# A list scheduler that counts results of other engines as ready somewhat later, with new due times

## The chip, the cores and the metric

The kernel runs on one core of a Trainium2 chip. A core has five engines that run side by side and wait for each other through semaphores: TensorE (PE in the profile; its weight loads are PEld), VectorE (DVE), ScalarE (ACT), GpSimd (POOL) and SyncE (SP), which here issues nearly all DMA transfers. The metric is the time of one execution on the device in microseconds, as the median of several runs.

## The reference

Four graph layers work on 128 graphs of 64 nodes, with 256 features a node, all in float32. Each layer adds to `x` a function of the normalized and rectified `h = max(layernorm(x), 0)`.

```python
# layers 0 and 1: attention of 8 heads over each graph; layer 0 masks, layer 1 adds log(adj + 1e-6)
attn = softmax(q @ k.T / sqrt(32) [masked or + log(adj + 1e-6)])
x = x + (attn @ v) @ Wo + bo
# layer 2: five rounds of a gated graph network
for l in range(5):
    m   = h @ weight[l]
    agg = A.T @ m                       # A = adj != 0, per graph
    h   = gru(agg, h)                   # gates r, z, n from 256 -> 768 products of agg and of h
x = x + h * mask
# layer 3: gated sum of a product along the graph and one beside it
f   = norm * (adj @ ((h @ theta) * norm))
g   = sigmoid(h @ W_t + b_t)
x   = x + elu(g * f + (1 - g) * (h @ W_h))
```

## The kernel before

**Tiling.** Two graphs make a tile of 128 rows (a pair), four pairs a group, and there are 16 groups. Activations of a group lie transposed, as two blocks of 128 features by 512 nodes. Products of 256x256 matrices are done with seven block products instead of eight (`by_seven`, `gru`, `seven_products`): sums of blocks are formed ahead on POOL or DVE, and each product's bank in PSUM is read by DVE or ACT before the next product goes into it. A second version of the whole network stands behind a branch that the run doesn't take; its instructions are in the program but do not run.

**The work of a group.** `front` does the two attention layers, in two halves of two pairs each: normalization (`norm_relu_t`: statistics and `xn` on DVE, the power on POOL, the turn `lnT` on TensorE, the copy `hT` on ACT), the products into `qkvb` and `qkvc`, the scores `s`, the exponential on ACT, the mask on POOL, the weighting `o` with its division on DVE, and the product `y`. `gru` does four rounds: the sums along the graph `agg`, their copy on ACT (L1063) and differences `Ta` on DVE (L1070), the products into `gb`, `gc`, `nb`, `nc`, the update on DVE, ACT and POOL (L1109 to L1130), and the turn `hT` of the new state. `last_step` does the fifth round by token, with additions of a bias row on POOL (L1209). `back` and `back_half` do layer 3: `lnT`, the products into `l3b` and `l3c` (in the last one and a half groups the plain products `f` and `gate`), `hom`, a chain of elementwise steps on DVE and ACT (L1478 to L1505), and the store.

**Small tiles.** Most matmuls use the whole array of TensorE. The scores `s` (L790) and sums `agg` (L1057) use tiles of 64x64, the weighting `o` (L858, L866) tiles of 64x32.

**The planner.** No instruction is written out in its final order. The program first adds operations to a `Plan` (`add`), each with its engine, an estimated cost and what it reads and writes. `Plan.run` then takes one operation after the other: of those that could start soonest on their engine, the one with the smallest due time, `op.key`. The order in which it takes them is the order of the instructions on each engine, and the buffers are given out in the same order. Four things steer it:

- `delay` (L195): how long after an operation's end its user on another engine may start, in the planner's count. `AFTER` holds the latencies by engine, `TO_PE` and `TO_POOL` additions.
- Due times: each stage is added within `plan.strand(base, span)`, which spreads the due times of its operations over `span` groups from `base`. The constants `FRONT`, `BACK`, `STEP`, `LOCK`, `ENTRY`, `FIRST`, `FUSE` and their like are these bases and spans.
- `shift` (L201): a bonus to small-tile work behind small-tile work (`BESIDE`), a malus for small-tile work that stands alone (`ALONE`), a bonus to transposes behind small-tile work (`TURNING`).
- `AHEAD`: how far ahead of the earliest due operation another may be taken.

So stages of up to four groups are interleaved on TensorE: while the GRU of one group runs, the attention of the next and layer 3 of the one before fill the gaps. Five products of weights for the rounds of the GRU (`fuse_weights`, `gv`) are made at the start, stored, and loaded again for each round.

Of the kernel before, what the change touches and what calls it, by code (L numbers as in the profile page):

```python
# [38 lines left out]

AFTER = {"PE": 210, "DVE": 125, "ACT": 145, "POOL": 90, "SP": 2500}  # L40
TO_PE, TO_POOL = 120, 60


HOLD = {"DVE": 60, "POOL": 95}
# [5 lines left out]

WIDE, T64, T32, TURN = range(4)
CHANGE = ((0, 95, 95, 0), (290, 0, 170, 190), (250, 135, 30, 150), (0, 95, 95, 0))
BESIDE = 0.52
ALONE = 0.17
TURNING = 0.46
AHEAD = 1.55

FRONT = 0.1  # L60
FRONT_LAST = 0.17
FRONT_SPAN = 1.03
BACK = 0.0
BACK_LAST = 0.43
BACK_SPAN = 0.7
STEP = -0.08
STEP_LAST = -0.07
STEP_SPAN = 0.4
LOCK = 0.23
BACK_END = 0.18  # L70
ENTRY = 0.63
FIRST = -1.31
FIRST_SPAN = 1.02
ORDER = (0, 0, 1, 0, 1, 0)
FUSE = -1.22
FUSE_SPAN = 0.33


WEIGH = (655, 1147)
# [57 lines left out]
class Plan:  # L137
# [56 lines left out]
    @staticmethod  # L194
    def delay(op, user):  # L195
        if user.eng == "PE":
            return 0 if op.eng == "PE" else op.lat + TO_PE
        return op.lat + (TO_POOL if user.eng == "POOL" and op.eng == "DVE" else 0)

    @staticmethod  # L200
    def shift(last, mode, small):  # L201

        if mode in (T64, T32):
            return -BESIDE if last in (T64, T32) else ALONE if small < 2 else 0.0
        return -TURNING if mode == TURN and last in (T64, T32) else 0.0

    def run(self):
# [12 lines left out]
        for _ in range(len(self.ops)):  # L220
            while due[0] in done:
                due.pop(0)
            best, horizon = None, due[0].key + AHEAD
            for eng, ops in ready.items():
# [64 lines left out]
def network(ctx: ExitStack, tc: tile.TileContext, a: dict, out: bass.AP, flag):  # L289
# [1066 lines left out]
    def entry(g, xt):  # L1356

        h = new("h", [P, 2, TOK], 3, f"h_{g}")
        ht = new("ht", [P, PAIRS, D], 3, f"ht0_{g}")
        for half in range(2):  # L1360
            norm_relu_t(xt, half, h, lambda half=half: h[:, :, half * HALF : (half + 1) * HALF],
                        [(h, (0, half)), (h, (1, half))], f"{g}_2_{half}", ht, seen=2 * g + half if lean else None)
        return h, ht

    def back(g, xt, norm):

        def fill():
            for gp in range(2):
                s = slice(gp * NODES, (gp + 1) * NODES)
                nc.sync.dma_start(blk[s, :, s], adj_t[s, g * PAIRS : (g + 1) * PAIRS, :])  # L1370

        dma(128, fill, [], [blk], 2)
        adjT = new("adjT", [P, PAIRS, P], 2, f"adjT_{g}")
        ps = bank(f"adjT_{g}")

        def turn():
            for p in range(PAIRS):
                nc.tensor.transpose(ps[:, p * P : (p + 1) * P], blk[:, p, :], ident.tile)

        pe(437, turn, [blk, ident], [ps], holds=[adjT], mode=TURN)  # L1380

        for p in range(PAIRS):
            sca(act(P, 1), lambda p=p: nc.scalar.activation(
                adjT[:, p, :], ps[:, p * P : (p + 1) * P], AF.Identity, scale=norm[:, p : p + 1]),
                [ps, norm], [(adjT, p)])
        for half in (0, 1) if g + 1 == n_groups else (1, 0):
            back_half(g, xt, adjT, norm, half)
# [126 lines left out]
    parts = {g: front(g) for g in range(n_groups)}  # L1514
    with plan.strand(FIRST, FIRST_SPAN):
        for g in ORDER:
# [6 lines left out]
    for l in range(LAYERS):  # L1523
        with plan.strand(FUSE + FUSE_SPAN * l, FUSE_SPAN):
            fuse_weights(l)
# [5 lines left out]
    taken = {g: ORDER.count(1) if g == 1 else 0 for g in range(n_groups)}  # L1531
    begin = {g: g - (LOCK if g + 1 == n_groups else 0.0) for g in range(n_groups)}
    events = sorted([(begin[g] + 0.4 * l, g, l) for g in range(n_groups) for l in range(LAYERS)] +
                    [(begin[g] - 1.001, g, -1) for g in range(1, n_groups)])
    for at, g, l in events:
        last = g + 1 == n_groups
        if l < 0:
            with plan.strand(begin[g] - 1 + FRONT + (FRONT_LAST if last else 0), FRONT_SPAN):
                for _ in range(4 - taken[g]):
# [7 lines left out]
        if l == 0:  # L1547
            xt, A, norm = held[g]
            with plan.strand(begin[g] + ENTRY, 0.1):
                h, ht = entry(g, xt)  # L1550
            held[g] = xt, norm
            chains[g] = gru(h, ht, A, g, last)
        with plan.strand(at + STEP + (STEP_LAST if last else 0), STEP_SPAN):
            next(chains[g])
        if l + 1 == LAYERS:
            with plan.strand(begin[g] + 2 + BACK + (BACK_LAST if g + 2 == n_groups else BACK_END if last else 0), BACK_SPAN):
                back(g, *held.pop(g))
# [52 lines left out]
```

## Time and profile before

| | |
|---|---|
| time, median of 3 runs | 2510.33 us (2509.15 to 2510.38) |
| profiled execution, its own time | 2510.45 us |
| span of the profiled execution, first to last instruction | 2508.4 us |
| TensorE busy | 2475.2 us in 23481 matmul records |
| weight loads busy | 2027.1 us |
| DVE busy | 1928.9 us |
| ACT busy | 1290.7 us |
| POOL busy | 992.0 us |
| granted TensorE clock, mean | 0.996 |

A float32 matmul instruction leaves two matmul records in the trace, a transpose one. Records overlap, since the next matmul starts before the last has ended; a record's length is therefore longer than its share of TensorE's time. In the timeline, the first column is the start in microseconds from the start of the span, the second the length, then engine, line, instruction, what is written and read, and `x4` for four records in a row.

The profile repeats: from the third group on, nearly every group takes the same time, about 152 us from one group's first `agg` to the next one's.

### The profile page before, as it was taken

The numbers are of one execution on the slowest core, as the hardware profiler recorded it, in microseconds if no ns is written. First come the engines' busy times: TensorE is split into PE (matmuls) and PEld (weight loads), VectorE is DVE, ScalarE is ACT, GpSimd is POOL, SyncE is SP. The second block draws the span as 40 slices with busy tenths as digits, with TensorE's granted clock in tenths as the row PEclk, the third lists the DMA queues.
The fourth block names the chain that finished last, engine by engine and source line by source line (L and its number), as shares of the span: only waits on it lengthen the run. The fifth ranks groups of instructions, "written<-read, shape, count | busy, mean of one in ns | idle before, by whom it ended". The sixth has DMA issues, their size and how long they took to land.

```text
span 2508.4 us, 58053 instructions
## 1 busy us (share of the span) xinstructions
PE 2475.2 (99%) x23481; PEld 2027.1 (81%) x23481; DVE 1928.9 (77%) x4524; ACT 1290.7 (51%) x2634; POOL 992.0 (40%) x959
## 2 busy tenths in 40 slices
PE   9999999999999999999999999999999999999997
PEld 7788788887878878788787888878788887887874
DVE  6676767878778797878878788797787878778676
ACT  3354454554555555454554545545455554554553
POOL 6633533525244243433524334253443434334242
PEclk9999999999999999999999999999999999999998
DMA  6421211222222122221322212222211222212210
GB/s 209 168 95 45 95 65 65 70 72 86 67 77 70 56 86 71 80 70 56 102 69 85 67 65 74 68 82 68 83 64 56 82 71 82 70 47 73 71 51 19
DMA packets 88601, 191.44 MB, mean 76 GB/s; under 512 B 23602, under 2 KB 77188, under 8 KB 77444
## 3 DMA queue, kind: packets, MB, share of 16 engines
q1 hardware_dynamic: 88208, 187.59, 22.4%
q8 instruction: 188, 3.08, 0.5%
q14 instruction: 89, 0.73, 0.1%
q10 hardware_dynamic: 116, 0.04, 0.0%
HBM read 169.58 MB, written 18.02 MB: 75 GB/s over the span
## 4 chain that ended last, share of the span: by engine, by line
PE 90%; DVE 8%; issue 1%; ACT 1%; POOL 0%; DMA 0%; DVEq 0%; ACTq 0%
PE gb L1012 17%; PE gc L1012 13%; PE nb L1012 9%; PE nc L1012 6%; PE qkvb L726 5%; PE y L894 5%; PE qkvc L726 4%; PE agg L1057 3%; PE l3b L1424 3%; PE gb L1194 3%; PE nb L1194 3%; PE s L790 2%; PE lnT L562 2%; PE l3c L1424 2%; PE hT L562 2%; PE o L858 2%
## 5 line engine op out<-in xcount | busy, mean ns | idle before, releaser
L1126 POOL TENSOR_TENSOR sn<-h,sn 128x512 f32<-128x512 f32 x128 | 165.0, 1289 | 670.6 <-ACT sn L1124 670.5
L548 POOL TENSOR_TENSOR rstd<-pw,few 128x2 f32<-128x2 f32 x128 | 103.8, 814 | 308.4 <-DVE pw L547 265.9
L981 POOL TENSOR_TENSOR Th<-h 128x256 f32<-128x256 f32 x160 | 119.1, 764 | 255.8 <-PE nb L1012 230.3
L814 POOL TENSOR_TENSOR e<-e,mask 128x512 f32<-128x512 f32 x128 | 177.8, 1406 | 80.4 <-ACT e L812 80.4
L1012 PE MATMUL gb<-Th,w_hh 128*128 128x256 f32 x768 | 197.6, 380 | 0.9 <-DVE sg L1089 0.9
L1012 PE MATMUL gb<-Ta,gv 128*128 128x256 f32 x768 | 197.3, 379 | 0.0
L1124 ACT ACTIVATE sn<-sn,b_n 128x512 f32<-128x512 f32 x128 | 92.3, 721 | 165.6 <-DVE sn L1122 164.5
L1012 PEld LDWEIGHTS gb<-Th,w_hh 128*128 128x128 f32 x768 | 142.5, 190 | 22.1 <-POOL rstd L548 1.3
L1012 PEld LDWEIGHTS gb<-Ta,gv 128*128 128x128 f32 x768 | 141.5, 190 | 19.8
L1109 ACT ACTIVATE sg<-sg,b_rz 128x512 f32<-128x512 f32 x128 | 87.9, 716 | 112.6 <-DVE sg L1089 112.6
L894 PE MATMUL y<-w_L_gnn_Wo,oT 128*128 128x256 f32 x512 | 142.8, 383 | 2.0 <-issue 1.6
L1128 DVE SCALAR_TENSOR_TENSOR sn<-sg,sn 128x512 f32<-128x512 f32 x128 | 105.9, 827 | 48.3 <-POOL sn L1126 48.3
L1070 DVE TENSOR_TENSOR Ta<-agg 128x256 f32<-128x256 f32 x160 | 90.8, 577 | 67.0 <-PE nb L1012 36.9
L1012 PE MATMUL gc<-h,w_hh 128*128 128x256 f32 x512 | 133.1, 382 | 0.1
L981 POOL TENSOR_TENSOR Th<-h,Th 128x256 f32<-128x256 f32 x160 | 128.3, 802 | 12.0 <-DVE h L1130 4.6
L1012 PE MATMUL gc<-agg,gv 128*128 128x256 f32 x512 | 131.5, 379 | 0.0
L726 PEld LDWEIGHTS qkvb<-hTQ,qw 128*128 128x128 f32 x696 | 101.5, 191 | 31.3 <-DVE v L747 11.4
L894 PEld LDWEIGHTS y<-w_L_gnn_Wo,oT 128*128 128x128 f32 x512 | 95.3, 190 | 30.0 <-issue 4.4
L803 POOL TENSOR_TENSOR x<-x,r_L_gnn_bo 128x512 f32<-128x512 f32 x64 | 83.1, 1299 | 85.7 <-DVE xn L592 74.6
L1012 PE MATMUL nb<-Th,w_hh 128*128 128x256 f32 x384 | 114.8, 381 | 0.0
L1012 PE MATMUL nb<-Ta,gv 128*128 128x256 f32 x384 | 114.5, 380 | 0.0
L726 PE MATMUL qkvb<-hTQ,qw 128*128 128x128 f32 x696 | 108.4, 278 | 4.7 <-DVE v L747 4.6
(286 smaller groups left out, 7070.6 us busy)
## 6 DMA issues: line engine op xcount, KB each, us to landing
gv<-gates SPq DMA_DIRECT2D x80, 1344.0 KB, 5.8
qw<-kept SPq DMA_DIRECT2D x203, 192.0 KB, 2.4
x<-in_x_dram SPq DMA_DIRECT2D x32, 256.0 KB, 2.9
out_dram<-x SPq DMA_DIRECT2D x32, 256.0 KB, 2.2
gates<-gv SPq DMA_DIRECT2D x5, 1344.0 KB, 5.0
adjq<-in_adj_dram SPq DMA_DIRECT2D x8, 256.0 KB, 3.5
adjblk<-in_adj_dram SPq DMA_DIRECT2D x32, 64.0 KB, 3.2
gw<-in_L_gnn_weight_dram SPq DMA_DIRECT2D x5, 256.0 KB, 5.9
```

Source lines behind the costliest of these rows:

```text
L548: pool(660 if n == 2 else 970, lambda: nc.gpsimd.tensor_tensor(dst.tile, s.tile, few[:, 1 : 1 + n], op=ALU.pow), [s, (few, 1)], [dst], port=2)
L562: nc.tensor.transpose(to, src_at(i), ident.tile)
L726: nc.tensor.matmul(bk[:, j * P : (j + 1) * P], lhs, rhs, start=first and j == 0, stop=True, skip_group_check=True)
L814: pool(1225, lambda e=e: nc.gpsimd.tensor_tensor(e.tile, e.tile, bias_at(pp)[:, None, :].to_broadcast([P, 4, 2 * NODES]), op=ALU.mult), [e ...
L894: pe(mm(256), lambda i=i, c=c: nc.tensor.matmul(py[:, i * D : (i + 1) * D], oT[:, i, c, :], w_o[:, c, :], start=c == 0, stop=c == 1), [(oT ...
L981: pool(690, lambda: nc.gpsimd.tensor_tensor(T[:, i, :], x(), y(), op=ALU.subtract), reads, [(T, i)])
L1012: nc.tensor.matmul(bank_[:, col * HALF : (col + 1) * HALF], at(g, n), rhs(), start=first and j == 0, stop=True, skip_group_check=True)
L1124: sca(act(TOK, 1.5), lambda: nc.scalar.activation(a_(), a_(), AF.Tanh, bias=b_n[:, oc : oc + 1]), [n_v, b_n], [n_v])
L1126: pool(1230, lambda: nc.gpsimd.tensor_tensor(b_(), hh(), a_(), op=ALU.subtract), [*hp, n_v], [n_v])
L1128: vec2(dve(TOK), lambda: nc.vector.scalar_tensor_tensor(b_(), z(), 1.0, b_(), op0=ALU.add, op1=ALU.mult), [*ts[1], n_v], [n_v])
L1194: pe(mm(384), lambda t=t, bk=bk: nc.tensor.matmul(bk[:, P:] if of_h else bk[:, : 3 * P], b()[:, t * P : (t + 1) * P], w[:, :, n, :], start ...
L1424: pe(mm(384), lambda: nc.tensor.matmul(bk[:, : 3 * P], b(), w3[:, :, n, :], start=first, stop=True, skip_group_check=True), [w3, *reads], ...
```

## The change

Three things change, all of them in what the planner counts with. A new constant `EASE = 60` is added in `delay` to the latency of each result of an engine other than TensorE, whoever uses it. The constants of the due times are set anew. The bonuses change: `BESIDE` from 0.52 to 0.78, `ALONE` from 0.17 to 0.07, `TURNING` from 0.46 to 0.14, and `AHEAD` from 1.55 to 1.25. No operation is added, removed or altered; costs of operations in the planner stay too.

```diff
 TO_PE, TO_POOL = 120, 60
+EASE = 60
...
-BESIDE = 0.52
-ALONE = 0.17
-TURNING = 0.46
-AHEAD = 1.55
+BESIDE = 0.78
+ALONE = 0.07
+TURNING = 0.14
+AHEAD = 1.25
...
-FRONT_LAST = 0.17
+FRONT_LAST = 0.25
...
-BACK_LAST = 0.43
+BACK_LAST = 0.35
...
-STEP = -0.08
-STEP_LAST = -0.07
-STEP_SPAN = 0.4
-LOCK = 0.23
-BACK_END = 0.18
-ENTRY = 0.63
-FIRST = -1.31
-FIRST_SPAN = 1.02
+STEP = 0.1
+STEP_LAST = -0.02
+STEP_SPAN = 0.35
+LOCK = 0.26
+BACK_END = 0.1
+ENTRY = 0.55
+FIRST = -1.33
+FIRST_SPAN = 1.08
...
-FUSE = -1.22
-FUSE_SPAN = 0.33
+FUSE = -1.25
+FUSE_SPAN = 0.2
...
         if user.eng == "PE":
-            return 0 if op.eng == "PE" else op.lat + TO_PE
-        return op.lat + (TO_POOL if user.eng == "POOL" and op.eng == "DVE" else 0)
+            return 0 if op.eng == "PE" else op.lat + TO_PE + EASE
+        return op.lat + EASE + (TO_POOL if user.eng == "POOL" and op.eng == "DVE" else 0)
```

A group is the unit of the due times: 0.1 is a tenth of a group. The second version of the network behind the branch is planned with the same constants.

## The prediction

> **What bounds the kernel now.** First the page: share of busy time, then the chain that ended last.
>
> ```profile
> span 2508.4 us, 58053 instructions
> ...
> PE 2475.2 (99%) x23481; PEld 2027.1 (81%) x23481; DVE 1928.9 (77%) x4524; ACT 1290.7 (51%) x2634; POOL 992.0 (40%) x959
> ...
> PE 90%; DVE 8%; issue 1%; ACT 1%; POOL 0%; DMA 0%; DVEq 0%; ACTq 0%
> ```
>
> TensorE (PE) bounds the span, and no DMA is on the chain. But matmul ends overlap, so "busy" hides lost time. I therefore take distances from one start to the next. The list of waits shows only the largest losses (total, times, longest):
>
> ```profile
> PE hom L1482 <- DVE F L1402: 5.4, 1, 5.4
> PE qkvb L726 <- DVE v L747: 4.6, 11, 1.5
> ```
>
> The PE timeline (start, length, instruction) gives prices:
>
> ```profile
> 1012.09 1.03 PE L1012 MATMUL gb<-Th,w_hh 128*128 128x256 f32 x4
> 1013.05 0.45 PE L858 MATMUL o<-e,v 64*32 64x64 f32 x32
> 1013.32 0.78 PE L866 MATMUL o<-e,ones 64*32 64x256 f32 x16
> 1013.75 0.66 PE L858 MATMUL o<-e,v 64*32 64x64 f32 x32
> 1014.34 1.13 PE L1012 MATMUL gc<-Th,w_hh 128*128 128x256 f32 x4
> 1015.31 1.03 PE L1012 MATMUL gc<-Ta,gv 128*128 128x256 f32 x4
> ...
> 1056.63 1.16 PE L1057 MATMUL agg<-A,ht 64*64 64x64 f32 x64
> 1057.61 1.06 PE L790 MATMUL s<-kexp,qk 64*64 64x128 f32 x32
> 1058.60 0.44 PE L1314 MATMUL mask<-ident,adjq 128*128 128x128 f32 x2
> ```
>
> Four 128x256 records cost 0.864 us between their own kind, but 0.957 ahead of small-tile work (1012.09 to 1013.05) and 0.968 behind it (1014.34 to 1015.31): 93 ns to enter, 104 to leave. A transpose behind it pays 55 (0.492 instead of 0.437). `o` is 1.288 whatever stands beside it. `agg` alone is 1.092 and `s` alone 1.034; joined they are 0.98 and 0.99 as above, so the pair saves about 160 ns besides one exit and entry. Other joins save only that exit and entry.
>
> With these prices I sum the order of TensorE's instructions as the program issues them: 2448.4 us, of it 44.5 on tile changes. The trace has 2495.3 from first to last matmul. The other 46.9 is waiting: 13.2 up to 338.7 us, 18.0 in the thirteen repeating groups from there to 2280.0, 15.7 after. A usual group lasts 152.06: 150.48 of sum and 1.58 of waiting. Ahead of the first matmul lie 1.35 us, behind the start of the last 11.7.
>
> Two places make 1.16 of the 1.58. DVE, then POOL, just there:
>
> ```profile
> 1202.38 1.16 DVE L1503 SCALAR_TENSOR_TENSOR o<-o,F 128x256 f32<-128x256 f32 x1
> 1203.46 0.28 DVE L747 TENSOR_TENSOR v<-qkvb,q 128x128 f32<-128x128 f32 x1
> 1203.66 1.28 DVE L1505 SCALAR_TENSOR_TENSOR x<-o,x 128x256 f32<-128x256 f32 x1
> 1204.87 1.76 DVE L1130 SCALAR_TENSOR_TENSOR h<-sn 128x512 f32<-128x512 f32 x1
> ```
>
> ```profile
> 1200.30 2.95 POOL L1209 TENSOR_TENSOR p<-p,b_row 128x512 f32<-128x512 f32 x2
> 1203.22 2.86 POOL L1209 TENSOR_TENSOR u<-u,b_row 128x512 f32<-128x512 f32 x2
> ```
>
> The medians of L1503, L1505 and L1130 over the run are 0.418, 0.422 and 0.682; here each lasts until a POOL addition ends. `v` stands behind L1503, and TensorE's last product into `qkvb` waits for `v`: 0.473 us, and 0.104 in the next instruction. `h` stands behind L1505, and the turn of `hT` waits: 0.186, 0.321 and 0.072 over three instructions. Together 1.16.
>
> **What the Trainium skill says.** "TensorEngine Tiling (Array Packing)", Key Properties: changing the tiling mode drains the engine; the 93 and 104 ns agree. "SBUF — State Buffer", Who interferes with whom: a VectorE instruction with two SBUF inputs and a GpSimd one that reads SBUF exclude each other, and the second waits for the first to finish; 1.16 instead of 0.42 agrees. "TensorE: Matmul & The Clock Gate", What's actually happening: an idle array gets a slower clock; in the last 133 us the clock was 0.93, and the matmuls from 2481.8 to 2486.5 took about twice their time.
>
> **The change, part by part.** No operation is added or removed; the 12321 matmul instructions and their 2404 us without tile changes stay. The 60 ns lie in the planner's head alone: they make it offer an operation later, so that other work goes first. All costs follow from the new order, which the built program shows on every engine.
>
> *Tile changes.* Runs of small-tile work, by count: before 152, of which 39 join `agg` and `s`, 13 `o` and `agg`, 4 `o` and `s`. After 163: 67 `agg` alone, 32 `s`, 19 `o`, 32 `o`+`s`, 13 `agg`+`o`; no pair of `agg` and `s` is left. 39 x 0.16 = 6.3; 11 more entries and exits x 0.197 = 2.2; 14 fewer exits into transposes x 0.049 = 0.7. Sum +9.1 us (44.5 to 53.65), 0.73 in each usual group, 8.8 of it in the middle stretch. This is bare TensorE time; nothing hides it. The pairs go although the bonus for small-tile work beside its like rises, since the new due times no longer bring `agg` and `s` up together.
>
> *The two waits of each group.* After, nothing stands between L745 and L747 at the same place of `qkvb` (before: L1503), nor between L1128 and L1130 of that step's `h` (before: L745, L1503, L747, L1505). The gap on TensorE between producer and waiting `qkvb` product grows from 1.94 to 2.10, and at the other three such places of a group nothing stands between L745 and L747 either. I take both waits as gone.
>
> *The other handoffs.* For each kind of way from a matmul over other engines back to a matmul I took the shortest response in the trace, and the matmul time that each order leaves for it. In a group of 233 TensorE operations, handoffs within 0.4 us of the shortest were 6 before and 4 after, within 0.6 us 13 and 9. None is below it. Before, most of the tightest came over DVE (`sg`, `h`), after over ACT (`agg`, `lnT`, `l3b`), which a POOL operation doesn't block; `agg` into `gb` has 0.14 over, and before one with 0.10 over did not wait. What remains I estimate at 0.3 us a group: between zero (no handoff falls short) and 1.58 (as many meet POOL as now). Middle stretch: 8.8 - 18.0 + 13 x 0.3 = -5.3.
>
> *DMA.* SP's queue is reordered too. From a free buffer to the first use of what is loaded into it lie at least 24.4 us for the `qw` blocks and 15.1 for `gv` before, 16.2 and 14.7 after; the page has them landing 2.4 and 5.8 us from issue. They stay hidden, and would cost nothing until over 8 us of that were lost.
>
> *Start.* The five fused weights are spread finer, and `y` and `qkvb` products stand further from their sources, but handoffs below the shortest response, the first five microseconds apart, sum to 1.7 us before and 4.4 after, while the real waiting before was 13.2, mostly queues on DVE. Taken at 0, from -6 (all but the first 3.3 and the new shortfalls gone) to +4.
>
> *End.* From the addition L1232 (2462.57) to the normalization of group 15's first half (L592, 2480.02) DVE runs 44 operations without a break, and TensorE waits. After, nine fewer stand there: those of group 14's layer 3, now in the 7.3 us in which DVE idled before L1232. By start distances: 2 x L1485 0.39, 1 each of L1478, L1488, L1490 0.34, 2 each of L1503 and L1505 0.33: 3.1 us. But the products that release L1232 end 22.4 us of matmul time before the end instead of 24.3: +1.9. Net -1.2. Against it, `lnT` of group 14 now has 15.4 us behind its last GRU product, and 18.9 is the shortest response seen; for it, three microseconds of GRU products stand between that `lnT` and `l3b`, which waited 1.04. I let these two cancel; from -4 to +4.
>
> Sum: 9.1 - 8.8 in the outer parts is +0.3; -5.3 + 0.3 + 0 - 1.2 = -6.2. Span 2502.2. The profiled execution took 2510.45, 2.05 more than its span, and is 0.1 above the median of 2510.33: hence 2504.1; I say 2504.
>
> **Rivals.**
> *Slower: waits form anew.* Now waits come where a two-input DVE operation meets POOL ahead of a short handoff. The order on each engine doesn't say when DVE and POOL meet, and a delay of 60 ns is small beside a POOL addition of 1.43. One hit per group costs 0.5 and its tail. With 13 groups, the middle stretch breaks even at 0.70 of waiting a group, and the kernel is slower by 5 us from about 1.15 on; at the old 1.58 it gains only the 1.2 of the end: 2510.3 + 9.1 - 1.2 = 2518. For it: DVE is busy 120.4 of 152 us in each group, so a queue is always near. Against it: the two old places are free now and the rest is wider.
>
> *A wash.* 0.75 us a group remain: +0.6 in the middle, -0.9 outside: 2510. For it: the new short `agg` handoffs; against: their like didn't wait.
>
> *More than forecast.* Waiting in the middle falls to 0.1 a group and the start sheds 4 us: 2504 - 2.6 - 4 = 2497. For it: the finer spread of the start; against: its new shortfalls.
>
> *The change doing nothing* is excluded: all five engines' orders differ.
>
> **How the numbers follow.** 0.2% (5 us, 2505.3 and 2515.4) is about what a measurement of this kernel can tell from no change. Forecast 0.57, own range 2498 to 2509: 0.45 faster, 0.12 same. More 0.11, faster. Wash 0.14: 0.13 same, 0.01 slower. Slower 0.18. So 0.56, 0.25, 0.19. The range takes the gain of the start down to 2495 and reaches up to 2516, part of the slower case, which leaves 2 in 10 outside.
>
> **What would show it.** Small-tile prices unchanged: `agg` all at 1.09, `s` 1.03, entries +93. Usual groups of 151.5 us instead of 152.06. The wait of `qkvb` for `v` reduced to a few at the start; `hT` not waiting in the repeating groups. At the end the wait of `hom` for `F` some microseconds, like now. I am wrong if groups last over 152.1: then a repeating wait has formed, and the list of waits or the start distances name it; or if the waits beyond 2280 us pass 20.

## The result, and the profile after

The changed kernel takes 2499.81 us, the median of 6 runs (2498.14 to 2500.03), against 2508.9 us (2507.66 to 2510.38) for the kernel before beside it. The ratio is 0.9961, with a 95% interval of 0.9948 to 0.9974. Measured again later (`after_again` below), it took 2498.6 against 2504.61: 0.9975, from 0.9967 to 0.9984. Both intervals lie below 1; the medians put the gain at 9.1 and at 6.0 us.

The profiled execution took 2500.02 us, with a span of 2498.1. First the page of the changed kernel, with the span, the busy time of each engine and the shares of the chain that ended last:

```profile
span 2498.1 us, 58019 instructions
...
PE 2472.3 (99%) x23481; PEld 2030.7 (81%) x23481; DVE 1911.6 (77%) x4524; ACT 1300.1 (52%) x2634; POOL 1009.7 (40%) x959
...
PE 97%; DVE 2%; ACT 1%; POOL 0%; issue 0%; DMA 0%; DVEq 0%; ACTq 0%
```

DVE's share of the chain falls from 8% to 2%. DVE executes the same 4524 instructions in 17.3 us less busy time, and that difference is telling: an instruction that is held counts as busy (L1503 stood in the trace of before with 1.16 us instead of 0.42), so the same work in less time means fewer or shorter holds. Next, the waits of TensorE in the changed kernel (line, releaser, total us, times, longest):

```profile
PE lnT L563 <- DVE xn L593: 4.8, 3, 3.4
PE hom L1483 <- DVE F L1403: 2.4, 1, 2.4
...
PE qkvb L727 <- DVE v L748: 0.3, 1, 0.3
```

The eleven waits of `qkvb` for `v` are one short wait now. `hT` waiting for `h` is gone from the list, where it stood with 1.3 us at two places of the first 340 us; the shorter waits of `hT` in each group are too short for this list. At the end `hom` waits 3.0 us less and `lnT` of group 15 some 3 us more. The TensorE timeline (start, length, instruction) at an `agg` that was joined to `s` before:

```profile
1057.11 0.81 PE L1195 MATMUL nb<-gv,Ta 128*128 128x384 f32 x2
1057.85 1.16 PE L1058 MATMUL agg<-A,ht 64*64 64x64 f32 x64
1058.94 0.71 PE L727 MATMUL qkvb<-hTQ,qw 128*128 128x128 f32 x4
```

From 1057.85 to 1058.94 are the 1.09 us of an `agg` that stands alone. Taking start distances as in the prediction, and the sum of TensorE's order at the same prices (the order sum), the two executions divide as follows (us, first to last matmul):

| | before | after | difference |
|---|---|---|---|
| order sum | 2448.4 | 2457.5 | +9.1 |
| waiting up to the first `agg` of group 2 (338.7 and 340.9) | 13.2 | 8.8 | -4.4 |
| waiting in the 13 repeating groups | 18.0 | 3.7 | -14.3 |
| waiting after them | 15.7 | 15.0 | -0.7 |
| first to last matmul | 2495.3 | 2485.1 | -10.3 |

A usual group lasts 151.40: 151.21 of sum and 0.19 of waiting. What happens now around the `h` of the same step is not what I had pictured. DVE, then POOL, then TensorE of the changed kernel:

```profile
1197.61 1.68 DVE L1129 SCALAR_TENSOR_TENSOR sn<-sg,sn 128x512 f32<-128x512 f32 x1
1199.39 1.57 DVE L1131 SCALAR_TENSOR_TENSOR h<-sn 128x512 f32<-128x512 f32 x1
1200.89 1.36 DVE L593 TENSOR_SCALAR xn<-x,mv,rstd 128x256 f32<-128x256 f32 x1
```

```profile
1197.47 2.95 POOL L1210 TENSOR_TENSOR p<-p,b_row 128x512 f32<-128x512 f32 x2
1200.38 3.00 POOL L1210 TENSOR_TENSOR u<-u,b_row 128x512 f32<-128x512 f32 x2
```

```profile
1201.11 0.81 PE L1195 MATMUL gc<-gv,agg 128*128 128x384 f32 x2
1201.75 0.60 PE L563 MATMUL hT<-ident,h 128*128 128x128 f32 x4
```

POOL's additions (L1210, which is L1209 before) still hold `h`, for 1.57 us. But only L1129 stands ahead of `h` in that stretch, so it is done at 1200.96 and `hT` follows at 1201.75 without waiting. The hold is covered, not avoided.

### The profile page after: what moved, and what is told of

Same layout as the page of the kernel before. It is cut to its first block, busy times and chain, and to the rows that moved or that the text cites. A ratio compares the mean times of both kernels' runs of the same rounds, so it can differ in the third digit from the quotient of the medians.

```text
span 2498.1 us, 58019 instructions
## 1 busy us (share of the span) xinstructions
PE 2472.3 (99%) x23481; PEld 2030.7 (81%) x23481; DVE 1911.6 (77%) x4524; ACT 1300.1 (52%) x2634; POOL 1009.7 (40%) x959
## 3 DMA queue, kind: packets, MB, share of 16 engines
q1 hardware_dynamic: 88208, 187.59, 22.5%
## 4 chain that ended last, share of the span: by engine, by line
PE 97%; DVE 2%; ACT 1%; POOL 0%; issue 0%; DMA 0%; DVEq 0%; ACTq 0%
PE gb L1013 18%; PE gc L1013 13%; PE nb L1013 9%; PE nc L1013 7%; PE qkvb L727 6%; PE qkvc L727 5%; PE y L895 4%; PE nb L1195 3%; PE agg L1058 3%; PE gb L1195 3%; PE l3b L1425 3%; PE s L791 3%; PE gc L1195 3%; PE nc L1195 2%; PE l3c L1425 2%; PE hT L563 2%
## 5 line engine op out<-in xcount | busy, mean ns | idle before, releaser
L815 POOL TENSOR_TENSOR e<-e,mask 128x512 f32<-128x512 f32 x128 | 170.2, 1342 | 237.9 <-ACT e L813 237.9
L982 POOL TENSOR_TENSOR Th<-h 128x256 f32<-128x256 f32 x160 | 125.5, 803 | 272.4 <-PE nb L1013 133.1
L549 POOL TENSOR_TENSOR rstd<-pw,few 128x2 f32<-128x2 f32 x128 | 114.2, 892 | 206.3 <-DVE pw L548 202.9
L1129 DVE SCALAR_TENSOR_TENSOR sn<-sg,sn 128x512 f32<-128x512 f32 x128 | 115.8, 905 | 45.9 <-POOL sn L1127 45.1
L982 POOL TENSOR_TENSOR Th<-h,Th 128x256 f32<-128x256 f32 x160 | 134.9, 843 | 8.9 <-DVE h L1131 5.9
L895 PE MATMUL y<-w_L_gnn_Wo,oT 128*128 128x256 f32 x512 | 133.3, 380 | 0.1
L804 POOL TENSOR_TENSOR x<-x,r_L_gnn_bo 128x512 f32<-128x512 f32 x64 | 89.4, 1397 | 77.9 <-DVE xn L593 52.5
L568 ACT ACTIVATE hT<-lnT 128x512 f32<-128x512 f32 x96 | 57.2, 596 | 116.9 <-PE lnT L563 116.9
L1064 ACT ACTIVATE agg<-agg 128x512 f32<-128x512 f32 x160 | 86.6, 593 | 58.9 <-PE agg L1058 58.8
L1090 DVE TENSOR_TENSOR sg<-gc,ug 128x512 f32<-128x512 f32 x64 | 43.8, 685 | 89.4 <-PE gc L1013 88.2
```

Of the source, the lines that this page charges most:

```text
L549: pool(660 if n == 2 else 970, lambda: nc.gpsimd.tensor_tensor(dst.tile, s.tile, few[:, 1 : 1 + n], op=ALU.pow), [s, (few, 1)], [dst], port=2)
L815: pool(1225, lambda e=e: nc.gpsimd.tensor_tensor(e.tile, e.tile, bias_at(pp)[:, None, :].to_broadcast([P, 4, 2 * NODES]), op=ALU.mult), [e ...
L895: pe(mm(256), lambda i=i, c=c: nc.tensor.matmul(py[:, i * D : (i + 1) * D], oT[:, i, c, :], w_o[:, c, :], start=c == 0, stop=c == 1), [(oT ...
L982: pool(690, lambda: nc.gpsimd.tensor_tensor(T[:, i, :], x(), y(), op=ALU.subtract), reads, [(T, i)])
L1129: vec2(dve(TOK), lambda: nc.vector.scalar_tensor_tensor(b_(), z(), 1.0, b_(), op0=ALU.add, op1=ALU.mult), [*ts[1], n_v], [n_v])
```

## The experiments

In each ratio the kernel before is the one that ran in the same comparison; its medians there were 2505.76 (`no_adds`, `behind_h`, `pad_only`, `due_only`), 2504.49 (`behind_sums`, `parted`, `no_pad`, `old_bonus`) and 2504.61 (`after_no_adds`, `v_first`, `after_again`, `pad_bonus`). The trace of before is an execution of 2510.45, above these, so I take ratios for the time and the traces for where it lies. Where an experiment reorders an engine, the planner first writes down its order, a function moves the named operations in that list, and only then is the code written; the added lines shift the line numbers, and the text says which line is which.

### Are POOL's additions what holds v and h?

The order of every instruction is kept, but the 108 additions are not issued (`no_adds` in the kernel before, `after_no_adds` in the changed one):

```diff
-                pool(1225, lambda c=c: nc.gpsimd.tensor_tensor(c.tile, c.tile, b_row[:, oc], op=ALU.add),
+                pool(1225, lambda: None,
                      [c, b_row], [c])
```

> The kernel before with the order of every instruction kept, but the POOL additions L1209 left out (108 of them: the bias rows in three of the products of the last GRU layer are not added). Theory A (these additions hold the two-input DVE operations ahead of v and h): L1503, L1505 and L1130 fall from 1.16, 1.28 and 1.76 us to about 0.42, 0.42 and 0.68 at those places, both waits go, about 15 us less, 2494. Rival B (the waits come from DVE's own queue): no more than 2 us less. If it is much below 2494, the additions also cost elsewhere, by lengthening the way from ACT's copies to the sums of the last layer.

Measured: 2499.06 us, ratio 0.9973 (0.9963 to 0.9984). DVE of `no_adds` at the old place:

```profile
1198.38 0.42 DVE L745 TENSOR_TENSOR qk<-qkvb,q 128x256 f32<-128x256 f32 x1 [0.64 <-PE qkvb L726]
1198.72 0.42 DVE L1503 SCALAR_TENSOR_TENSOR o<-o,F 128x256 f32<-128x256 f32 x1
1199.06 0.28 DVE L747 TENSOR_TENSOR v<-qkvb,q 128x128 f32<-128x128 f32 x1
1199.26 0.42 DVE L1505 SCALAR_TENSOR_TENSOR x<-o,x 128x256 f32<-128x256 f32 x1
1199.59 0.68 DVE L1130 SCALAR_TENSOR_TENSOR h<-sn 128x512 f32<-128x512 f32 x1
```

L1503, L1505 and L1130 take 0.42, 0.42 and 0.68, as theory A said. A usual group waits 0.54 instead of 1.58, and the waiting of the thirteen groups falls from 18.0 to 7.0. So the additions are the cause of 1.04 us per group; theory B falls. The size was less than the 15 us expected: the groups gave 11.0, and `nb` behind `hT` still waits 0.09 and 0.07.

> The changed kernel with the order of every instruction kept, but POOL's additions L1210 (L1209 before) left out, 108 of them: the bias rows in three of the products of the last GRU layer are not added. Taken out of the kernel before, they were worth 1.04 us of waiting per repeating group. Theory A (in the new order they meet nothing that TensorE waits for): the middle stretch is the same within 2 us (waiting 3.7), the ratio to before that of the changed kernel. Rival B (they still cost, and the rest of the gain came from elsewhere): some 5 us or more below the changed kernel.

Measured: 2498.28 us, ratio 0.9979 (0.997 to 0.9987), beside 0.9975 for the changed kernel in the same comparison; waiting in the groups 3.3, beside 3.6. The same additions that cost 1.04 us a group in the old order cost nothing that can be measured in the new one. Theory A stands. So the additions account for some 1.0 of the 1.39 us of waiting that a usual group loses by the change; what made up the rest was not taken apart.

### Can the old order be mended by moving the two operations?

Three kernels change DVE's list at the twelve places. In the rules below "late" marks L1503 and L1505, "h" L1130, and "sum" the last of the four sums L1220 that follow `h`; the output DMA that reads what L1505 writes moves along with it.

`v_first` puts `v` ahead of L1503:

```diff
+    for last, op in zip(dve, dve[1:]):
+        if last.mark == "late" and op.mark == "v":
+            put_behind(order, [last], op, {"DVE"})
```

> The kernel before with one swap on DVE at the twelve places: v (L747) ahead of L1503 instead of behind it, nothing else moved. Theory A (v waits only for L1503, and L1503 only for POOL's addition L1209): the 0.473 us of qkvb and the 0.104 of the next instruction go at each place, h keeps its time, because L1503, L1505 and L1130 are still held by the same additions: 12 x 0.58 = 6.9 us less, ratio 0.9972, groups of 151.5. Rival B (TensorE, 0.58 us earlier, only waits that much longer for h or for a bank): 0 to 2 us less, ratio 0.9995, with a longer wait of hT for h or a new one of nb.

Measured: 2512.08 us, ratio 1.0037 (1.0023 to 1.0052). The waits of TensorE in `v_first`, then its DVE (L1540, L1543 and L1166 are L1503, L1505 and L1130):

```profile
PE hT L596 <- DVE h L1166: 9.4, 14, 1.0
...
PE qkvb L760 <- DVE v L781: 1.5, 1, 1.5
```

```profile
1201.80 0.28 DVE L781 TENSOR_TENSOR v<-qkvb,q 128x128 f32<-128x128 f32 x1
1202.00 1.51 DVE L1540 SCALAR_TENSOR_TENSOR o<-o,F 128x256 f32<-128x256 f32 x1
1203.55 1.37 DVE L1543 SCALAR_TENSOR_TENSOR x<-o,x 128x256 f32<-128x256 f32 x1
1204.84 1.76 DVE L1166 SCALAR_TENSOR_TENSOR h<-sn 128x512 f32<-128x512 f32 x1
```

The wait of `qkvb` is gone from the groups, and `hT` waits 0.86 us, with 0.32 behind it, where it had waited 0.19 and 0.32 (and 0.07 after). A group still lasts 152.15. `h` is done when POOL has finished, whatever TensorE did before: rival B by its mechanism, though the ratio is above the 0.9995 that it named. The two waits of the prediction were one delay, paid at two places.

`behind_h` puts L1503 and L1505 (collected in `between`) behind `h`:

```diff
+        elif op.mark == "h":
+            if between:
+                put_behind(order, between, op)
```

> The kernel before with its order kept on every engine except DVE: at the twelve places where L1503 and L1505 stand between L1128 and L1130, both are put behind L1130, so that v (L747) and h (L1130) no longer stand behind them. Leaves nothing out. Theory A (the 1.16 us of waiting per repeating group come from these two operations, each held by a POOL addition L1209 ahead of v and h): 12 x 1.16 = 13.9 us less, about 2495; the wait of qkvb for v shrinks from 11 times to the few of the start, and hT no longer waits for h; groups of 150.9 instead of 152.06. Rival B (the waits come from how late DVE is there altogether, not from these two): no change, 2509. Rival C (the meeting with POOL only moves on to the next operations, L1220 of the last layer, and TensorE then waits for the sums): between 2500 and 2509, with a wait of another name in each group.

Measured: 2512.98 us, ratio 1.0026 (1.0015 to 1.0036). The waits of `behind_h`, then its DVE (L1171 is L1130, L1545 and L1548 are L1503 and L1505, L1262 is L1220):

```profile
PE nb L1052 <- DVE pw_deg L587: 11.4, 12, 1.0
```

```profile
1205.62 1.22 DVE L1171 SCALAR_TENSOR_TENSOR h<-sn 128x512 f32<-128x512 f32 x1
1206.76 1.49 DVE L1545 SCALAR_TENSOR_TENSOR o<-o,F 128x256 f32<-128x256 f32 x1
1208.29 1.38 DVE L1548 SCALAR_TENSOR_TENSOR x<-o,x 128x256 f32<-128x256 f32 x1
1209.59 0.41 DVE L1262 TENSOR_TENSOR sg<-gc,u 128x256 f32<-128x256 f32 x1
```

Neither `v` nor `h` is waited for in the groups any more, but the sums of the last layer now stand behind the two held operations, and the next product into `nb` waits 1.08 us and 0.07 in the next instruction. The trace names `pw_deg` (L587) as what released it; that operation of 0.15 us stands directly behind the first two sums. This is rival C by its mechanism, to the size of the old wait, though the time lies above its 2500 to 2509. A group lasts 152.06.

`behind_sums` carries them past the sums as well:

```diff
+        elif op.mark == "sum" and beyond:
+            put_behind(order, beyond, op, {"DVE", "SP"})
```

> The kernel before with L1503 and L1505 of the twelve places put still further back: behind L1130, the copy L573 and the four sums L1220 that stand there, where DVE idled 0.79 us ahead of L1254; TensorE, ACT and POOL keep their order, one DMA of the output goes behind one load of qw. Theory A (what costs is any two-input DVE operation that waits for POOL's additions L1209 ahead of v, h and the sums that free a bank; behind these it is harmless): waiting per repeating group from 1.58 to about 0.45 with a sum of 2448.4, so 13 to 14 us less than before, ratio 0.9945, faster than the change itself. Rival B (h itself, L1130, still meets L1209 and takes 1.2 us, and what follows is late all the same): as the first of these orders, which only moved the wait to nb: ratio 1.000 to 1.003.

Measured: 2522.83 us, ratio 1.0076 (1.0063 to 1.009), so both theories missed. L1503 and L1505 take 0.41 and 0.42 there, and the sums are in time. What became late is a load. DVE of `behind_sums` (L1550 is L1505) and its DMA issues on SP:

```profile
1212.51 0.42 DVE L1550 SCALAR_TENSOR_TENSOR x<-o,x 128x256 f32<-128x256 f32 x1
...
1219.80 0.75 DVE L627 BATCH_NORM_STATS2 st<-x 128x6 f32<-128x256 f32 x2 [4.67 <-DMA x<-in_x_dram]
```

```profile
1212.97 0.39 SPq L1553 DMA_DIRECT2D out_dram<-x  x1
1216.92 0.90 SPq L403 DMA_DIRECT2D x<-in_x_dram  x2
```

The next `x` is loaded into the buffer that the output leaves. In the kernel before that output was issued at 1204.97, the load at 1207.20, and the statistics found it without idle time. Here the load comes at 1216.92, DVE stands for 4.67 us with everything behind it, and TensorE waits 1.92 us for the sums (`gb`) and 1.07 at `gc` in this group. So L1505 has little room between POOL's additions and the next load of `x`. None of the three moves made the old kernel faster, and each lost to another neighbour: `h`, the sums, the load.

### Is the price of the parted pairs right?

`parted`, in the kernel before, swaps `s` with the next operation of TensorE wherever it follows `agg`:

```diff
+    for last, op, at in zip(pe, pe[1:], pe[2:]):
+        if last.mode == T64 and op.mode == T64 and op.vals[-1].name[:2] != "ag" and op not in at.users:
+            put_behind(order, [op], at, {"PE"})
```

> The kernel before with one swap on TensorE at 24 places: where s follows agg, the next operation (a transpose of mask 12 times, a product of gc 12 times) goes between the two. Every other engine keeps its order. By the prices of the prediction: 24 x 0.16 for the lost joint, 24 more exits and entries, of which 12 with a transpose: tile changes 44.5 to 53.1, so +8.6 us, ratio 1.0034, and groups 0.71 longer. Rival B (the pair saves little of itself, its price was read from too few places): +3 us or less. Rival C (a parted s is late for its softmax, or gc comes earlier and takes the waits with it): more than +12 or less than +4 with changed waits.

Measured: 2524.3 us, ratio 1.0078 (1.0064 to 1.0092). TensorE of `parted` at one place of each kind:

```profile
1251.55 1.16 PE L1091 MATMUL agg<-A,ht 64*64 64x64 f32 x64
1252.64 1.13 PE L1046 MATMUL gc<-h,w_hh 128*128 128x256 f32 x4
1253.70 1.10 PE L824 MATMUL s<-kexp,qk 64*64 64x128 f32 x32
1254.73 1.13 PE L1046 MATMUL gb<-agg,gv 128*128 128x256 f32 x4
...
1366.19 1.16 PE L1091 MATMUL agg<-A,ht 64*64 64x64 f32 x64
1368.06 0.44 PE L1348 MATMUL mask<-ident,adjq 128*128 128x128 f32 x2 [0.70 <-ACT agg L1097]
```

Where `gc` goes between, the start distances are 1.092, 1.061 and 1.035: the prices of the prediction to a few nanoseconds, with 0.864 + 0.104 + 0.093 for `gc`. The order sum over these is 2457.0, +8.6. Where the transposes of `mask` go between, they come 0.77 us too soon for what ACT has to copy first, a wait that `s` had covered; twelve of these are 9.2 us. Part of that takes the place of other waiting (`qkvb` for `v` falls from 4.6 to 3.6): in all the waiting rises by 5.4, and first to last matmul is 14.0 longer. The price of the pairs is confirmed; rival C is right that a swap costs more than its price.

### Which part of the change does it?

The change has three parts: the pad of 60 ns, twelve due times and four bonuses. `pad_only` and `due_only` are the kernel before with one part of the change. `no_pad`, `old_bonus` and `pad_bonus` are the changed kernel with one part put back, in this order:

```diff
-EASE = 60
+EASE = 0
```

```diff
-BESIDE = 0.78
-ALONE = 0.07
-TURNING = 0.14
-AHEAD = 1.25
+BESIDE = 0.52
+ALONE = 0.17
+TURNING = 0.46
+AHEAD = 1.55
```

```diff
-FRONT_LAST = 0.25
+FRONT_LAST = 0.17
...
-STEP = 0.1
+STEP = -0.08
...
-FUSE_SPAN = 0.2
+FUSE_SPAN = 0.33
```

> The kernel before with the 60 ns alone: every due time and bonus as before. Its order on TensorE has 177 runs of small-tile work (152 before, 163 after the whole change) and 53.9 us of tile changes instead of 44.5, so a sum of 2457.8 from first to last matmul. In its order L1503 no longer stands between L745 and L747 at the last place of a group, but stands between L1128 and L1130 of one step. Theory A (the pad makes the order that spares the waits; the due times add little): waits of some 27 us as after the whole change, about 2500. Theory B (it is the due times that part the DVE operations; the pad only breaks up the pairs): the waiting stays near 47, about 2518.

> The kernel before with the new due times alone: no pad, the four bonuses as before. 158 runs of small-tile work, 51.5 us of tile changes instead of 44.5, a sum of 2455.4. No DVE operation of L1503 or L1505 stands ahead of v or h at the old two places. Theory A (the pad is what spares the waits): waiting near 47 as before, about 2516. Theory B (the due times do it): waiting near 27 as after the whole change, about 2498, faster than with the pad by the 2.2 us of fewer tile changes.

> The changed kernel without the 60 ns: new due times and new bonuses alone. Tile changes 53.5 us, sum 2457.4, as with the pad (2457.5). Theory A (the pad parts short handoffs; without it they fall short): waits above 40, 2512 or more, ratio 1.002 or more. Theory B (due times and bonuses together make the order, the pad decides little): waits near 27, 2499, ratio 0.996.

> The changed kernel with the four bonuses as before (pad and due times new). Tile changes 52.2 us, sum 2456.1, 1.4 less than after the whole change. Theory A (pad and due times together spare the waits, the bonuses do nothing for them): waits near 27, ratio 0.9955. Theory B (every part of the change gives another order, and only the one that was found together is good): waits above 40, ratio 1.001 or more.

> The kernel before with the pad and the new bonuses, but the due times as before. Tile changes 51.3 us, sum 2455.2, 2.4 less than after the whole change. No pair of L1503 and v. Theory A (pad and bonuses make the good order): waits near 27, 2497, ratio 0.995. Theory B (without the due times the DVE operations still stand ahead of v and h at POOL's additions, as with the pad alone, where qkvc waited 0.54 in each group): waits of 45 to 55, ratio 1.003 to 1.007.

Measured, with the waiting from the start distances of each trace and DVE's busy time from each page:

| parts new | us | ratio (interval) | order sum | waiting: start, groups, end | DVE busy |
|---|---|---|---|---|---|
| none | | 1 | 2448.4 | 13.2, 18.0, 15.7 | 1928.9 |
| pad | 2524.84 | 1.0083 (1.007 to 1.0097) | 2457.8 | 12.9, 22.5, 16.3 | 1960.3 |
| pad, bonuses | 2532.96 | 1.0117 (1.0101 to 1.0133) | 2455.1 | 11.4, 32.2, 18.3 | 1979.1 |
| due times | 2520.15 | 1.0058 (1.0044 to 1.0071) | 2455.4 | 11.9, 19.7, 18.1 | 1910.5 |
| due times, pad | 2509.74 | 1.002 (1.0013 to 1.0027) | 2456.1 | 13.4, 10.5, 15.7 | 1920.3 |
| due times, bonuses | 2512.1 | 1.0029 (1.0017 to 1.0041) | 2457.4 | 14.1, 13.0, 14.4 | 1919.9 |
| all | 2499.81 | 0.9961 (0.9948 to 0.9974) | 2457.5 | 8.8, 3.7, 15.0 | 1911.6 |

Every one of these orders costs TensorE 6.7 to 9.4 us more than the old one, and only the one with all three parts saves more waiting than that. Waiting in all is 51.7 with the pad alone and 49.6 with the due times alone, so there the theories of "near 47" hold and neither part does it alone. Without the pad it is 41.5, without the new bonuses 39.6: both less than before and far from 27. With pad and bonuses but without the new due times it is 62.0, worse than either theory had it. With the new due times the pad takes 9.2 us off the groups' waiting without the bonuses and 9.3 with them, and the bonuses take 6.7 without the pad and 6.8 with it; without the due times pad and bonuses only add. DVE's busy time goes with the due times: with them it is 1910 to 1920, without them 1929 to 1979 for the same 4524 instructions, so it is they that lower how long DVE is held. That alone does not spare TensorE's waits: the due times alone have the lowest busy time of the table, 1910.5, and their groups wait 19.7.

With the pad alone the old mechanism shows at another place. The waits of `pad_only`, DVE, and POOL (L711, a difference for `hTQ`, stands between L746 and L748, the sums that the `qkvc` product waits for):

```profile
PE qkvc L727 <- DVE v L748: 4.2, 11, 0.4
```

```profile
1198.25 0.42 DVE L746 TENSOR_TENSOR qk<-qkvc,q 128x256 f32<-128x256 f32 x1 [0.22 <-PE qkvc L727]
1198.59 1.40 DVE L711 TENSOR_TENSOR hTQ<-hT,hTQ 128x128 f32<-128x128 f32 x1
1199.91 0.28 DVE L748 TENSOR_TENSOR v<-qkvc,q 128x128 f32<-128x128 f32 x1
```

```profile
1198.58 1.26 POOL L1210 TENSOR_TENSOR p<-p,b_row 128x512 f32<-128x512 f32 x1
```

0.54 us are lost at that product and 0.10 behind it. This is not the whole failure: a group of `pad_only` waits 1.73 us on average, and in every second group up to the ninth some 2 us more are lost at `lnT`, `gb`, `gc`, `hT` and once more at `qkvc`, which were not followed. What the pad removes when the due times are new is of another kind. In a usual group of `no_pad` (0.95 to 0.98 of waiting) the losses are small and many: 0.18 at two turns of `hT`, 0.10 at a third, and 0.04 to 0.10 at five more products. With the pad a single 0.105 stands above 0.04. In the prediction's words these are handoffs that are just short. That the planner without the pad counts them as met is the likely reason, but its counts were not looked at. What the bonuses change in the waits was not followed up, and the bonuses alone were not run.

### Do the outer stretches come back?

> The changed kernel once more, beside the runs of this call, for its second profile. If the waits of the first 340 us (8.8 against 13.2 before) and of the last stretch (15.0 against 15.7) follow from the order, they come back within 0.5 us; if they are chance of one execution, they scatter by some us as the loads do. Ratio 0.996.

Measured: 2498.6 us, ratio 0.9975 (0.9967 to 0.9984). Waiting: 7.4 at the start, 3.6 in the groups, 15.6 at the end. The start moves by 1.4 us between two executions and the end by 0.6, more than expected, but the start does not move to where the old order is: the six executions with the start of the kernel before (before, the three moves, `no_adds`, `parted`) wait 11.7 to 15.2 there, the three with the new one (`after_no_adds` with 7.1 among them) 7.1 to 8.8. The gain at the start belongs to the order. Its size is 3 to 8 us by these ranges, and 5.5 from mean to mean. None of the five orders made from parts of the change has it: they wait 11.4 to 14.1 there, one execution each.

## Why the prediction was right, and where it was off

The forecast of 2504 with a gain was right in sign, and 2499.81 lies 4.2 below it, in the range. Against the trace of before the sum was -6.2 and the trace shows -10.3. That the second comparison gave a gain of 6.0, as if the sum had been exact, is chance: there the kernel before ran some 6 us faster than in the trace from which the forecast starts.

**Tile changes.** Predicted +9.1, of it 0.73 in each usual group. The order has it, single `agg` and `s` stand at 1.092 and 1.035 us, and `parted` showed the prices at places where nothing else changed. Right.

**The two waits of each group.** Predicted gone, 1.16 of 1.58; they are gone, and the groups wait 14.3 less (predicted 14.1). Two things in the reasoning were wrong. First, I added the waits of `v` and `h` as two; `v_first` and `behind_h` showed one delay behind POOL that the next handoff collects when an earlier one is freed. Of the 0.321 us that I booked on the turn of `hT`, 0.27 stood ahead of the product into `nb`, which waits for what stands behind `h` on DVE; that is the wait that `behind_h` made long. Adding the two did no harm to the sum because the changed order frees all of them. Second, I wrote that nothing stands between L745 and L747 at the other three places of a group. That is wrong: in twelve groups L1122 (L1123 now) stands there at one of them, at 1097.17 for example. It takes 0.68 us, its usual time: POOL had been idle for 8 us or more at all twelve places, and its next operation (L982) starts 0.26 us behind L1123. The argument has to be who meets POOL and with how much cover, not who stands between: `h` is still held for 1.57 us in the new order and costs nothing.

**The other handoffs.** Estimated at 0.3 us a group, between 0 and 1.58; measured 0.19. The range of this estimate was where the real risk lay: the same kind of order gave 0.95 (`no_pad`), or 1.81 in every second group up to the ninth (`old_bonus`). What I assumed of ACT held in the trace of before: its copy `hT` (L567) took 0.597 us in the median both with a POOL operation running and without. "Slower: waits form anew" did not come to pass, but five orders made from parts of the same change did just that: their groups wait 0.8 to 2.5 us on average, above the 0.70 at which the middle stretch breaks even. Nothing in my working would have told these from the good one, since it did not place DVE and POOL against each other in time.

**DMA.** Nothing was lost, as said. But I looked at `qw` and `gv` alone. `behind_sums` shows that `x` is the load with little to spare: L1505 sets when it can be issued.

**Start.** This is the step that failed: predicted 0 (-6 to +4), measured -4.4, and -5.8 in the second profile. I weighed shortfalls in the order, 1.7 us before and 4.4 after, although the text itself said that most of the real 13.2 were queues on DVE. Single waits of the old start were 1.66 us (`qkvb`, at 117.9), 1.20 (`hT`, 170.2) and 1.91 (`y`, 209.0); ahead of the second, L1128 and L1130 took 1.79 and 1.57 beside POOL's L814. DVE, POOL and TensorE of the kernel before at that place:

```profile
166.72 1.79 DVE L1128 SCALAR_TENSOR_TENSOR sn<-sg,sn 128x512 f32<-128x512 f32 x1
168.61 1.57 DVE L1130 SCALAR_TENSOR_TENSOR h<-sn 128x512 f32<-128x512 f32 x1
```

```profile
166.69 2.94 POOL L814 TENSOR_TENSOR e<-e,mask 128x512 f32<-128x512 f32 x2
```

```profile
170.24 0.66 PE L562 MATMUL hT<-ident,h 128*128 128x128 f32 x4 [1.04 <-DVE h L1130]
```

In the changed kernel no single wait from 60 us to the end of this stretch is above 0.63. The shortfalls that I counted for the new order showed, if at all, as five waits of 0.3 to 0.6 us. In the traces this term accounts for the miss. The rival "More than forecast" had named it, 4 us shed at the start, with a chance of 0.11. Its reason was the finer spread of the fused weights. The constants of that spread (`FUSE`, `FUSE_SPAN`) are due times, and with the due times alone the start waits 11.9, so they do not do it alone. Why only the whole change sheds these waits stays open.

**End.** Predicted -1.2 (-4 to +4). Waiting fell by 0.7, and by 0.2 in the second profile. The 17.45 us of the prediction ran from L1232 to the end of the normalization (L592, 2480.02). DVE before and after at that place:

```profile
2479.29 0.73 DVE L592 TENSOR_SCALAR xn<-x,mv,rstd 128x256 f32<-128x256 f32 x2
```

```profile
2469.47 0.73 DVE L593 TENSOR_SCALAR xn<-x,mv,rstd 128x256 f32<-128x256 f32 x2 [0.60 <-POOL rstd L549]
```

From L1233 (2454.95) to the same end (2470.20) DVE now takes 15.25 us, 2.2 less (predicted 3.1): the nine operations are gone, but it idles for 0.60 us, since POOL's `rstd` is not ready. And TensorE stands in the same stretch for 2.56 (`hom`) and 3.67 (`lnT`), together 6.2 as before (5.61 and 0.58): the wait moved to the operation behind it, because the products come to their end earlier as well. For group 14, `l3b` waits 0.1 instead of 1.04 and a product of `gb` behind `lnT` 0.94 more, so these two cancel, as I let them.

**The time around the span.** The 2.05 us were 1.9 in the profiled execution of the changed kernel. The 0.1 by which the trace of before stood above its median was not typical: its later medians are 5 to 6 us below that execution. In its trace two of thirteen groups wait only 0.60 and 0.86, and in `parted`, whose DVE and POOL keep the old order, `qkvb` waits for `v` at seven of the twelve places only; so not every execution need meet POOL in each group. That this makes its time vary is a guess, for no second trace of it was taken, and where these 5 us lie stays open. The ratios of `v_first` and `behind_h`, 1.0037 and 1.0026 for spans that are 1.4 and 4.2 us above that of the trace of before, must be read with this.

## What to carry to other kernels

When an engine is held by another, follow the delay to its last user: a wait that is taken from one handoff is collected by the next, until there is cover or the order frees them all; a held operation with enough matmul time behind it costs nothing. Busy time of the same instructions (here DVE's, 1929 to 1912) shows at a glance whether an order has fewer of these meetings, but not whether it is faster: it was 1910.5 with the due times alone and 1887.1 in `behind_sums`, and both were slower than the kernel before. Constants of a planner that were set together should be judged together: here pad and due times alone, and every two of the three parts together, made the kernel slower, and only the whole made it faster, while the work that the new order adds for sure (here 9.1 us of tile changes) can be counted beforehand.

## What the runs showed of the hardware

A run of DVE operations with two inputs in SBUF does not merely wait once for POOL's pair of additions: behind the two pairs of L1209, of 2.95 and 2.86 us, four that follow one another (L1128, L1503, L1505, L1130) each take 1.2 to 1.8 us instead of 0.42 to 0.69. Between them `qk` and `v` (L745, L747), which read one operand from PSUM, keep their 0.41 and 0.28 us. A normalization (L593) with one tensor input is held like the two-input operations, 1.36 us instead of 0.41. That fits the Trainium skill, "SBUF — State Buffer", Who interferes with whom, which counts `tensor_scalar` among the operations that can take the shared port pair in a faster mode; in which mode L593 ran no run here shows.
